# Decoder layer in fp32: a feed-forward bias of six rows in four row groups, reciprocal parts on ScalarE, correction product first, second unit reordered

## Chip, cores and metric

The kernel runs on one core of a Trainium2 chip. The metric is the device time of one execution in microseconds (us). Five engines work side by side, each with its own queue: TensorE (PE, with its weight loads shown as PEld), VectorE (DVE), ScalarE (ACT), GpSimd (POOL) and SyncE (SP, which here issues most of the DMAs). An engine works through its queue in order.

## The reference

One decoder layer on x (8 x 256 tokens of 512 features), all in fp32:

```python
x = layernorm(x + self_attention(x))     # 16 heads of 128, RoPE, causal
x = layernorm(x + cross_attention(x, ctx))  # 16 heads of 32, mask, residual scale, its own norm
x = layernorm(x + ffn(x))
```

Self-attention uses a signed weight, `sign(s) * exp(|s| - max|s|)`, over its absolute sum. The feed-forward part quantises activations and weights:

```python
xq = clip(round(x * 127 / max|x|), -128, 127) / (127 / max|x|)   # one scale for each token
wq = clip(round(w / mean|w|), -1, 1) * mean|w|                   # one scale for each matrix
h = gelu(xq @ w1q.T + b1)        # 512 -> 2048
h = layernorm(h) * gamma + beta
y = quantised(h) @ w2q.T + b2    # 2048 -> 512
```

## The kernel before, in words

The 2048 tokens are 16 tiles of 128. The work has two phases.

**Self-attention** is 32 units, 8 pairs of heads times 4 pairs of batches. fp32 matrices are split in a high and a low part and multiplied in three matmuls (L146 to L148, `mm3`); the split of an x or a weight is a cast (high part, L156 or L185) and a subtraction (low part, L157 or L183). The order of work of a unit is a string of marks (`SCHED["unit"]`, L60 to L71): `Q` and `V` are projections, `s` scores, `S` the softmax's start, `x` its exponentials, `N` its normalisation (DVE, `e`, L419), `t` the transposes of the weights (PE, L426), `u` and `r` parts of RoPE, `R` its sum, and so on; a digit says which head or half. Several units are interleaved in one string. `emit` walks through it. Marks like `X0`, `XA`, `XB`, `X1`, `BY`, `BW`, `G1` are places at which `background` (L522 to L611) hangs work for later units: loads and splits of the next x, splits of the next weights. `X0` splits the first half of the next x on DVE (L156, L157), `XA` does the cast of its second half on ACT (L185) and `XB` or `X1` the subtraction on DVE (L183). The second unit, `ui == 1`, has its own string, made from the general one by replacements (L633 to L637).

**Everything after** (from about 920 us) is written as steps, `S(...)`, each with one or more choices of engine, a planned cost, and the tiles that it reads and writes. A list scheduler puts the steps in order by due times (`PLAN`, L38 to L58); planned costs, due times and engine choices are constants in the code. The order that results is then binding on each engine (`in_order`, L1355). Three kinds of steps interleave:

- Cross-attention of a batch (L854 to L1011): scores (PE, L880), exponentials (ACT, L884), mask (DVE, L888), products with v and denominators (PE, L895, L911), reciprocals (DVE, L921; `rs` L923), their spread over the heads (PE `rp`, L930), the product with it (DVE, L933), split (`cT`, L951, L952), output projection (PE `xo`, L146 to L148), and for each tile a norm, residual, second norm (`acc`, L980) and the quantisation for the feed-forward part: `absmax` (DVE, L985 to L987), `inverse` (POOL, L993 to L1001), `acc * scale + magic` (ACT, L1004), clip to bf16 (DVE, L1008), transpose by DMA (SP, xT<-xq) and store to DRAM (`xqs`). L827 and L831 (PE `tp`, DVE `x1T`) transpose and split the next queries' x.
- The feed-forward tables (L1014 to L1048): quantised weights, gamma, beta, and the bias table `b1s`, built in four blocks on DVE (L1034, L1036).
- The feed-forward part of a tile (L1050 to L1162): `up` (PE, L1070, and its bias L1071), Gelu (ACT, L1075), mean (DVE, L1080), squares (ACT, L1084), rstd (POOL, L1089 to L1091), scale and shift in halves (DVE L1095 and L1108; ACT L1103, DVE or POOL L1105, POOL L1107), absolute maximum (DVE, L1111), `scale` (DVE, L1116 to L1118), quantisation to `hq` (L1124, L1125), transpose by DMA (SP, hT<-hq), `down` (PE `dn`, L1131, and the correction product, L1133), last residual and norm.

How the bias gets in: `up` accumulates integers times the weights' signs, and Gelu multiplies by the token's scale `a1s`. So b1 has to be divided by that scale. The reciprocal of a token's scale is cut in three bf16 parts, and b1 too. The parts of the reciprocal lie in columns of `xq` (512 to 639) that the DMA transposes with the rest, and so become rows of the fifth block of `x2`. Before, the first part stands in rows 0, 32 and 64 of that block, the second in 33 and 65, the third in 66, all others being zero, and `b1s` has 96 rows: 32 with the third part of b1, 32 with the second, 32 with the first. One matmul of 96 rows for each 512 columns (L1071) adds the six products.

How the correction gets in: `hq` is stored shifted by `HALF`, and `unhalf` times the column sums `csum` takes that out again; before, after the 16 products of `down`.

Of the kernel before, what the change touches and what calls it, by code (L numbers as in the profile page):

```python
# [10 lines left out]
F32 = mybir.dt.float32  # L11
# [67 lines left out]
def decoder_kernel(ctx: ExitStack, tc: tile.TileContext, a, out):  # L79
# [28 lines left out]
    def T(tag, shape, dt=F32, name=None):  # L108
        return (keep if tag in ("w", "xt") else sb).tile(shape, dt, name=name or tag, tag=tag, bufs=BUFS.get(tag, 1))
# [412 lines left out]
    def background(ui):  # L522
# [6 lines left out]
        if nx is not None and nx.hp == 0:  # L529
            if ui == 0:  # L530
                ex["BA"].append(nx.xload)
            ex["X0" if ui < 2 else "B0"].append(lambda: nx.xsplit(0))
            ex["XA"].append(lambda: x_half(nx.xt, nx.raws[1], 1, 0, nc.scalar))
            ex["XB" if ui > 1 else "X1"].append(lambda: x_half(nx.xt, nx.raws[1], 1, 1, nc.vector))
        elif nx is not None:
            ex["BA"].append(nx.load)
        if ui < 2:
# [6 lines left out]
        for n, hp, k1 in ([("wO", u.hp, "BW")] if ui else [], [] if ui > 1 else [("wO", 0, "BW")], [("wQ", u.hp + 1, "BW")], [("wK", u.hp + 1, ""), ("wV", u.hp + 1, "")])[u.bp]:  # L544
            if (ui or n == "wO") and hp < NHP:
                raws = {}
                ex["BV" if n == "wV" else "BA"].append(lambda n=n, hp=hp, raws=raws: raws.update(w=raw_load(a[n][hp])))
                if n == "wV":
                    late["wv"] = raws
                elif n == "wK":  # L550
                    def hi(raws=raws, hp=hp):
                        w = hw.setdefault(hp, {})["wK"] = T("w", [128, 2, 1024], F32R)
                        half_split(w[:, 0], w[:, 1], raws["w"], 0, nc.scalar)

                    def lo(raws=raws, hp=hp):
                        w = hw[hp]["wK"]
                        half_split(w[:, 0], w[:, 1], raws["w"], 1, nc.vector)

                    ex["G0"].append(hi)
                    ex["BX"].append(lo)  # L560
                else:
                    ex[k1].append(lambda n=n, hp=hp, raws=raws: load_hp(hp, n, raws["w"]))
        if ui in ABS:
# [67 lines left out]
    for ui, u in enumerate(units):  # L631
        spec = SCHED["unit" if ui else "first"]
        if ui == 1:  # L633
            for old, new in ((" N0 XB", ""), (" n0 m1", " n0 N0 m1"), ("Q000 s00 Q001", "Q000 Q001 s00"), (" S0 BA", " S0 BA f0- f2-"),
                             (" V0 v0", ""), (" t00", " V0 v0 t00")):
                assert old in spec
                spec = spec.replace(old, new, 1)  # L637
        emit(spec, u, units[ui - 1] if ui > 0 else None, units[ui - 2] if ui > 1 else None, background(ui))
        if ui == 0:
            in_order(["PE", "Activation", "DVE", "Pool", "SP"])  # L640
# [120 lines left out]
        nc.scalar.activation(mv[:, 1:2], mv[:, 6:7], AF.Identity, scale=1.0 / D)  # L761

    def rstd(mv):
        nc.gpsimd.tensor_scalar(mv[:, 2:3], mv[:, 1:2], EPS, None, ALU.add)
        nc.gpsimd.tensor_tensor(mv[:, 3:4], mv[:, 2:3], nhalf, ALU.pow)

    def shift(mv):
# [86 lines left out]
    def x(b):  # L854
# [80 lines left out]
        for qi in range(2):  # L935
# [29 lines left out]
            def scale1(m1=m1):  # L965
# [9 lines left out]
              rd=[m1, A], wr=[d])  # L975
            S([("DVE", 0.8, lambda d=d, m2=m2: stats(H[d], H[m2])),
               ("ACT", 2.1, lambda d=d, m2=m2, xq=xq: astats(H[d], H[m2], H[xq][:, 0:512]))], rd=[d], wr=[m2, f"{xq}/q"], new=[m2] + new(xq))
            S([("POOL-", 1.0, lambda m2=m2: rstd(H[m2]))], wr=[m2])
            S([("DVE", 0.13, lambda m2=m2: shift(H[m2]))], wr=[m2])
            S([("ACT", 0.71, lambda tt=tt, d=d, m2=m2: nc.scalar.activation(acc[:, tt], H[d], AF.Identity, bias=H[m2][:, 2:3], scale=H[m2][:, 3:4]))],  # L980
              rd=[d, m2], wr=[A])
# [6 lines left out]

            S([("DVE", 0.85, absmax)], rd=[A], wr=[f"{m2}/s"])

            def inverse(tt=tt, m2=m2, xq=xq):
                s, xq = H[m2], H[xq]
                nc.gpsimd.tensor_tensor(a1s[:, tt : tt + 1], s[:, 10:11], wscale[:, 0:1], ALU.mult)  # L993
                nc.gpsimd.memset(xq[:, 512:640], 0.0)
                inv = s[:, 12:13]
                nc.gpsimd.tensor_tensor(inv, s[:, 11:12], wscale[:, 2:3], ALU.mult)
                for n in (3, 2, 1):
                    c0 = 512 + 33 * (3 - n)
                    nc.gpsimd.tensor_copy(xq[:, c0 : c0 + 32 * n - 31 : 32], inv.to_broadcast([128, n]))
                    if n > 1:  # L1000
                        nc.gpsimd.tensor_tensor(inv, inv, xq[:, c0 : c0 + 1], ALU.subtract)  # L1001

            S([("POOL-", 2.0, inverse)], rd=[f"{m2}/s"], wr=[f"{xq}/i", f"a1s:{tt}"], new=new(xq))
            S([("ACT", 0.71, lambda tt=tt, d=d, m2=m2: nc.scalar.activation(H[d], acc[:, tt], AF.Identity, bias=magic, scale=H[m2][:, 11:12]))],  # L1004
              rd=[A, f"{m2}/s"], wr=[d])
            S([(e, us, lambda tt=tt, g=g: g.tensor_tensor(acc[:, tt], acc[:, tt], H["b2b"], ALU.add))
               for e, us, g in (("POOL", 1.3, nc.gpsimd), ("DVE+", 0.65, nc.vector))], rd=["b2b"], wr=[A])
            S([("DVE+", 0.36, lambda d=d, xq=xq: nc.vector.tensor_scalar(H[xq][:, 0:512], H[d], MAGIC + 127.0, -MAGIC, ALU.min, ALU.add))],  # L1008
# [5 lines left out]
    def ffn_tables():  # L1014
        unit[0] = ("w", 0)
        for wi in range(2):
            key = f"fw{wi}"
            mk(key, "xt", [128, 8192], (BF16, F16)[wi])
            for c in range(4):
                cs = slice(2048 * c, 2048 * c + 2048)  # L1020
                load(key, wq_s[wi][:, cs], 2.8, rd=["ks3:0"], part=f"/{c}", f=lambda t, cs=cs: t[:, cs])
        for n in ("g2", "be2"):
            mk(n, "w", [128, 2048])
            load(n, a[n].to_broadcast([128, 2048]), 5.0, rd=["ks2:3"])
        mk("b1s", "w p4", [96, 2048], BF16)
        for c in range(4):
            r, cs = f"b1r{c}", slice(512 * c, 512 * c + 512)
            mk(r, "p2", [96, 512])
            load(r, a["b1"][:, cs].to_broadcast([96, 512]), 1.1, rd=["ks2:3"])

            def rows(r=r, cs=cs):
                t, b1s = H[r], H["b1s"]
                for n in (96, 64, 32):
                    nc.vector.tensor_copy(b1s[0:n, cs], t[0:n])  # L1034
                    if n > 32:
                        nc.vector.tensor_tensor(t[0 : n - 32], t[0 : n - 32], b1s[0 : n - 32, cs], ALU.subtract)  # L1036
# [12 lines left out]

    def ffn(tt):  # L1050
# [10 lines left out]
        for g in range(2):  # L1061
            ps = f"up{tt}{g}"
            bank(ps, "D", [128, 1024])

            def up(g=g, ps=ps):
                for c in range(2):
                    o = H[ps][:, 512 * c : 512 * c + 512]
                    f0 = 1024 * g + 512 * c
                    for k in range(4):
                        nc.tensor.matmul(o, H[x2][:, k], H["fw0"][:, 2048 * k + f0 : 2048 * k + f0 + 512], start=k == 0, stop=False)  # L1070
                    nc.tensor.matmul(o, H[x2][0:96, 4], H["b1s"][:, f0 : f0 + 512], start=False, stop=True)  # L1071

# [40 lines left out]

        def scale():
            s = H[st]
            nc.vector.tensor_tensor(s[:, 8:9], s[:, 8:9], s[:, 9:10], ALU.max)  # L1116
            nc.vector.tensor_scalar(s[:, 8:9], s[:, 8:9], EPS, 1.0 / 127.0, ALU.max, ALU.mult)
            nc.vector.reciprocal(s[:, 9:10], s[:, 8:9])  # L1118

        S([("DVE", 0.3, scale)], rd=[f"{st}/x{e}" for e in range(2)], wr=[f"{st}/s"])  # L1120
# [6 lines left out]
        bank(dn)  # L1127

        def down(ks_):
            for k in ks_:  # L1130
                nc.tensor.matmul(H[dn], H[hT][:, k], H["fw1"][:, 512 * k : 512 * k + 512], start=k == 0, stop=False)  # L1131
            if 15 in ks_:
                nc.tensor.matmul(H[dn], unhalf, csum, start=False, stop=True)  # L1133

        fw1 = [f"fw1/{c}" for c in range(4)]
        if tt in PLAN["dve"]:
# [288 lines left out]
```

## Time and profile before

| | us |
|---|---|
| three runs, median (lowest to highest) | 1386.69 (1386.09 to 1386.78) |
| the profiled execution's own time | 1387.89 |
| its span | 1386.1 |

| engine | busy, us | share of the span | instructions |
|---|---|---|---|
| PE | 1346.7 | 97% | 8576 |
| DVE | 1091.8 | 79% | 2040 |
| ACT | 880.4 | 64% | 1948 |
| POOL | 782.0 | 56% | 985 |

The span is that of the profiled execution, from its first to its last instruction; the difference of 1.8 us to its time lies around it. Times in views of the profile count from the span's start. In the order-of-time view a line has the start, the busy time (of several instructions of the same kind, if it ends in a count over 1), the engine, the line of the code, the operation, out<-in with shapes, and in brackets idle time ahead of it and what ended that. A view of stretches gives the busy time of each engine in a piece of the span, then the granted TensorE clock as a share of the full one, the share of DMA and GB/s. A view of waits names what an engine waited for: the total, how often, and the longest.

### The profile page before, as it was taken

The page shows a single profiled execution, that of the slowest core. Times are in us where ns is not written, and L with a number is a line of the kernel's source. Part 1 is how long each engine was busy: PE and PEld are TensorE (multiplying, and loading weights), DVE is VectorE, ACT ScalarE, POOL GpSimd, SP SyncE. Part 2 cuts the span into 40 slices and gives each one's busy share as a digit, 9 for nine tenths or more (in the row PEclk, how much of TensorE's full clock was granted, in tenths as well). Part 3 has the DMA queues.
Part 4 walks back from the last instruction along what each step waited for, and adds up shares of the span by engine and source line. Part 5 has one row for each costly group of instructions (what it writes and reads, how often), then busy time and mean ns, then how long its engine had stood idle before and what let it go on. Part 6 is the DMA issues. An engine that isn't in the chain of part 4 may idle for free.

```text
span 1386.1 us, 23778 instructions
## 1 busy us (share of the span) xinstructions
PE 1346.7 (97%) x8576; PEld 1081.0 (78%) x8576; DVE 1091.8 (79%) x2040; ACT 880.4 (64%) x1948; POOL 782.0 (56%) x985
## 2 busy tenths in 40 slices
PE   9899999999999999999999999999999999988896
PEld 7789988898889888998889888888667667543342
DVE  6877768778767888887877876868767877798997
ACT  4666776776776666666665666633644445576995
POOL 5656556656666666766665665525033324376764
PEclk9999999999999999999999999999999999999999
DMA  8442342234322244223422342225324424214453
GB/s 309 182 185 109 116 178 107 92 114 165 121 76 96 92 143 176 104 84 124 189 88 99 126 175 107 69 99 191 114 59 126 140 68 143 86 34 94 113 116 99
DMA packets 85046, 170.13 MB, mean 123 GB/s; under 512 B 47040, under 2 KB 57024, under 8 KB 80064
## 3 DMA queue, kind: packets, MB, share of 16 engines
q1 hardware_dynamic: 82624, 165.99, 35.1%
q10 hardware_dynamic: 2304, 2.62, 0.7%
q8 instruction: 68, 1.11, 0.3%
q14 instruction: 50, 0.41, 0.1%
HBM read 130.31 MB, written 27.79 MB: 114 GB/s over the span
## 4 chain that ended last, share of the span: by engine, by line
PE 82%; DVE 10%; POOL 3%; ACT 2%; issue 2%; DMA 1%; SPq 0%; POOLq 0%; ACTq 0%; DVEq 0%
PE ppj L146 12%; PE ppj L147 12%; PE ppj L148 12%; PE pz L146 3%; PE pz L148 3%; PE pz L147 3%; PE pwt L426 3%; PE sc L880 3%; PE den L911 2%; PE av L895 2%; PE ppo L146 2%; PE ppo L147 2%; PE ppo L148 2%; PE psc L376 2%; PE pz L449 2%
## 5 line engine op out<-in xcount | busy, mean ns | idle before, releaser
L324 POOL TENSOR_TENSOR sw<-sw,stab 128x512 f32<-128x512 f32 x128 | 170.2, 1329 | 101.5 <-ACT sw L315 101.0
L146 PE MATMUL ppj<-xt,w 128*128 128x512 f32 x528 | 209.0, 396 | 0.3 <-ACT xt L285 0.3
L147 PE MATMUL ppj<-xt,w 128*128 128x512 f32 x528 | 206.5, 391 | 1.0 <-DVE xt L157 0.4
L148 PE MATMUL ppj<-xt,w 128*128 128x512 f32 x528 | 206.2, 391 | 0.0
L146 PE MATMUL ppj<-w,xt 128*128 128x256 f32 (+1 forms) x528 | 157.2, 298 | 1.1 <-DVE u L320 1.1
L348 POOL TENSOR_TENSOR rh<-u,rh 128x512 fp32r<-128x512 f32 x64 | 97.6, 1526 | 99.8 <-PE ppj L148 88.2
L148 PE MATMUL ppj<-w,xt 128*128 128x256 f32 (+1 forms) x528 | 152.0, 288 | 0.0
L147 PE MATMUL ppj<-w,xt 128*128 128x256 f32 (+1 forms) x528 | 151.9, 288 | 0.0
L320 DVE SCALAR_TENSOR_TENSOR u<-ppj,bqk,ctab 128x512 f32<-128x512 f32 x128 | 95.5, 746 | 70.9 <-ACT sw L315 70.6
L314 ACT ACTIVATE sw<-ppj,bqk 64x512 f32<-64x512 f32 x128 | 87.8, 686 | 92.7 <-PE ppj L148 87.9
L332 POOL TENSOR_TENSOR u<-u,sw 128x256 f32<-128x256 f32 (+1 forms) x128 | 130.8, 1022 | 0.3 <-DVE u L320 0.2
L419 DVE SCALAR_TENSOR_TENSOR e<-aw,rd,sg 128x128 f32<-128x128 f32 (+1 forms) x256 | 126.3, 550 | 0.1
L148 PEld LDWEIGHTS ppj<-xt,w 128*128 128x128 f32 x528 | 99.2, 188 | 21.6 <-DVE w L183 0.4
L406 ACT ACTIVATE aw<-aw,nm 128x256 f32<-128x256 f32 (+1 forms) x256 | 113.2, 443 | 3.9 <-DVE nm L397 3.9
L391 POOL TENSOR_SCALAR_AFFINE_SELECT aw<-aw 128x256 f32<-128x256 f32 x128 | 59.9, 492 | 98.7 <-ACT aw L385 98.7
L453 ACT CAST z<-pz 128x512 fp32r<-128x512 f32 x64 | 37.6, 587 | 121.3 <-PE pz L449 121.3
L147 PEld LDWEIGHTS ppj<-xt,w 128*128 128x128 f32 x528 | 99.3, 188 | 17.9 <-DVE xt L183 0.8
L146 PEld LDWEIGHTS ppj<-xt,w 128*128 128x128 f32 x528 | 99.3, 188 | 17.1 <-ACT xt L285 0.7
L146 PEld LDWEIGHTS ppj<-w,xt 128*128 128x128 f32 x528 | 101.9, 193 | 2.0 <-DVE u L320 1.4
L147 PEld LDWEIGHTS ppj<-w,xt 128*128 128x128 f32 x528 | 102.0, 193 | 0.6
L148 PEld LDWEIGHTS ppj<-w,xt 128*128 128x128 f32 x528 | 101.7, 193 | 0.7
L385 ACT ACTIVATE aw<-psc 128x384 f32<-128x384 f32 x128 | 62.3, 487 | 60.6 <-PE psc L148 59.9
(283 smaller groups left out, 3937.0 us busy)
## 6 DMA issues: line engine op xcount, KB each, us to landing
xt<-xs SPq DMA_DIRECT2D x28, 2048.0 KB, 8.2
xs<-xt SPq DMA_DIRECT2D x4, 2048.0 KB, 12.9
raw<-w1T SPq DMA_DIRECT2D x16, 512.0 KB, 9.5
raw<-w2T SPq DMA_DIRECT2D x16, 512.0 KB, 9.6
acc<-xn SPq DMA_DIRECT2D x4, 1024.0 KB, 8.5
raw<-wO SPq DMA_DIRECT2D x8, 512.0 KB, 9.6
wq<-wqt SPq DMA_DIRECT2D x16, 256.0 KB, 2.4
kx<-ks SPq DMA_DIRECT2D x8, 512.0 KB, 4.9
```

Of the source, the lines that this page charges most:

```text
L146: nc.tensor.matmul(ps, lh, rh, start=first, stop=False)
L147: nc.tensor.matmul(ps, lh, rl, start=False, stop=False)
L148: nc.tensor.matmul(ps, ll, rh, start=False, stop=last)
L314: nc.scalar.activation(sw[0:64], ps[64:128], AF.Identity, bias=bias[64:128])
L320: nc.vector.scalar_tensor_tensor(v3(u), v3(self.ps.pop((h, i))), self.bias(h, i), ctab.to_broadcast([128, 2, 256]), ALU.add, ALU.mult)
L324: nc.gpsimd.tensor_tensor(v3(sw), v3(sw), stab.to_broadcast([128, 2, 256]), ALU.mult)
L332: nc.gpsimd.tensor_tensor(u, u, sw, ALU.add)
L348: (nc.gpsimd if i else nc.vector).tensor_tensor(lo, u if i else u[:, :, 128:256], f32(hi), ALU.subtract)
L385: nc.scalar.activation(aw[:, h], sc3, AF.Abs, scale=1.0 / math.sqrt(DH))
L391: nc.gpsimd.affine_select(aw[:, :, blk], aw[:, :, blk], pattern=[[0, 2], [-1, 128]], compare_op=ALU.is_ge, fill=MASKED, base=0, channel_mu ...
L406: nc.scalar.activation(aw[:, h, blk], aw[:, h, blk], AF.Exp, bias=nm[:, h, i : i + 1], accum_out=rd[:, h, i : i + 1])
L419: nc.vector.scalar_tensor_tensor(e[:, h, blk], aw[:, h, blk], rd[:, h, i : i + 1], sg[:, h, blk], ALU.mult, ALU.mult)
```

## The change

1. **Second unit.** In the string of `ui == 1`, the split of the first half of the next x (`X0`) goes from behind `R00` to behind `N1`, the cast of the second half (`XA`) behind `H11`, its subtraction from `X1` to `BY`; `N0`, `L00` and `u10` go ahead of `m1`, and `x0` ahead of `H00`. The split of wO in this unit becomes two parts, the cast on ACT at `G1` and the subtraction on DVE at `BW`.
2. **Bias table.** b1 lies in rows 32c to 32c + 31 for the columns 512c to 512c + 511 (c = 0 to 3), so `b1s` is 128 x 512 with 528 columns of work space in place of 96 x 2048. In each group six rows hold parts of b1: rows 1, 3, 5 the first part, 2 and 4 the second, 0 the third. Masks for these rows are sums of columns of the identity.
3. **Reciprocal parts.** They are made on ACT, in the step after L1004, six columns in each of four groups. The POOL step stays in the plan with nothing in it; its memset moves into the step `rstd` of the same tile.
4. **Up.** The bias product of 512 columns uses six rows of its row group; both of a half come behind the eight other products.
5. **Down.** The correction product comes first.
6. **Small ones.** `rstd`: add EPS becomes times 1.0 plus EPS. `scale`: a maximum of two and a maximum with EPS become one instruction, the multiplication another.

The planned costs, due times and engine choices stay as they are, and so does the order of the steps on each engine.

```diff
-            ex["XB" if ui > 1 else "X1"].append(lambda: x_half(nx.xt, nx.raws[1], 1, 1, nc.vector))
+            ex["XB" if ui > 1 else "BY" if ui else "X1"].append(lambda: x_half(nx.xt, nx.raws[1], 1, 1, nc.vector))
...
-                elif n == "wK":
+                elif n == "wK" or ui == 1:
...
-                    ex["G0"].append(hi)
-                    ex["BX"].append(lo)
+                    ex["G0" if n == "wK" else "G1"].append(hi)
+                    ex["BX" if n == "wK" else "BW"].append(lo)
...
-            for old, new in ((" N0 XB", ""), (" n0 m1", " n0 N0 m1"), ("Q000 s00 Q001", "Q000 Q001 s00"), (" S0 BA", " S0 BA f0- f2-"),
+            for old, new in ((" N0 XB", ""), (" L00 n0 m1", " n0 N0 L00 u10 m1"), (" H01 u10 R10", " H01 R10"), (" H00 x0 a11 XA", " x0 H00 a11"), (" R00 X0", " R00"), (" N1 X1", " N1 X0"),
+                             (" l0 k10 k11 BX", " XA l0 k10 k11 BX"), ("Q000 s00 Q001", "Q000 Q001 s00"), (" S0 BA", " S0 BA f0- f2-"),
...
-        nc.gpsimd.tensor_scalar(mv[:, 2:3], mv[:, 1:2], EPS, None, ALU.add)
+        nc.gpsimd.tensor_scalar(mv[:, 2:3], mv[:, 1:2], 1.0, EPS, ALU.mult, ALU.add)
...
-            S([("POOL-", 1.0, lambda m2=m2: rstd(H[m2]))], wr=[m2])
+            def rstd_zero(m2=m2, xq=xq):
+                rstd(H[m2])
+                nc.gpsimd.memset(H[xq][:, 512:640], 0.0)
+
+            S([("POOL-", 1.0, rstd_zero)], wr=[m2])
...
-                nc.gpsimd.tensor_tensor(a1s[:, tt : tt + 1], s[:, 10:11], wscale[:, 0:1], ALU.mult)
-                nc.gpsimd.memset(xq[:, 512:640], 0.0)
+            S([("POOL-", 2.0, lambda: None)], rd=[f"{m2}/s"], wr=[f"{xq}/i", f"a1s:{tt}"], new=new(xq))
+
+            def rounded(tt=tt, d=d, m2=m2, xq=xq):
+                s, s_xq = H[m2], H[xq]
+                xq4 = s_xq[:, 512:640].rearrange("p (g r) -> p g r", g=4)
+                nc.scalar.activation(H[d], acc[:, tt], AF.Identity, bias=magic, scale=s[:, 11:12])
                 inv = s[:, 12:13]
-                nc.gpsimd.tensor_tensor(inv, s[:, 11:12], wscale[:, 2:3], ALU.mult)
-                for n in (3, 2, 1):
-                    c0 = 512 + 33 * (3 - n)
-                    nc.gpsimd.tensor_copy(xq[:, c0 : c0 + 32 * n - 31 : 32], inv.to_broadcast([128, n]))
+                nc.scalar.activation(inv, s[:, 11:12], AF.Identity, scale=wscale[:, 2:3])
+                for c0, n in ((0, 3), (3, 2), (5, 1)):
+                    nc.scalar.copy(xq4[:, :, c0 : c0 + n], inv.rearrange("p (g r) -> p g r", g=1).to_broadcast([128, 4, n]))
                     if n > 1:
-                        nc.gpsimd.tensor_tensor(inv, inv, xq[:, c0 : c0 + 1], ALU.subtract)
+                        nc.scalar.activation(inv, s_xq[:, 512 + c0 : 513 + c0], AF.Identity, scale=-1.0, bias=inv)
+                nc.scalar.activation(a1s[:, tt : tt + 1], s[:, 10:11], AF.Identity, scale=wscale[:, 0:1])
...
-            load(r, a["b1"][:, cs].to_broadcast([96, 512]), 1.1, rd=["ks2:3"])
+            r, ps_ = f"b1r{c}", slice(32 * c, 32 * c + 32)
+            mk(r, "p2", [128, 512])
+            load(r, a["b1"][:, 512 * c : 512 * c + 512].to_broadcast([32, 512]), 1.1, rd=["ks2:3"], f=lambda t, ps_=ps_: t[ps_])
...
-                for n in (96, 64, 32):
-                    nc.vector.tensor_copy(b1s[0:n, cs], t[0:n])
-                    if n > 32:
-                        nc.vector.tensor_tensor(t[0 : n - 32], t[0 : n - 32], b1s[0 : n - 32, cs], ALU.subtract)
+                t, b1s, part, m = H[r][ps_], H["b1s"][ps_, 0:512], H["b1s"][ps_, 512:1024], H["b1s"][ps_, 1024:1040]
+                for i, rs_ in enumerate(((1, 3, 5), (2, 4), (0,))):
+                    mi = m[:, 4 * i : 4 * i + 2].bitcast(F32)
+                    nc.vector.tensor_reduce(mi, ident[ps_, rs_[0] : 128 : 32], AX.X, ALU.add)
+                    for q_ in rs_[1:]:
+                        nc.vector.tensor_reduce(m[:, 12:14].bitcast(F32), ident[ps_, q_ : 128 : 32], AX.X, ALU.add)
+                        nc.vector.tensor_tensor(mi, mi, m[:, 12:14].bitcast(F32), ALU.add)
+                    nc.vector.tensor_copy(part, t)
+                    if i < 2:
+                        nc.vector.tensor_tensor(t, t, part, ALU.subtract)
+                    if i:
+                        nc.vector.scalar_tensor_tensor(b1s, part, mi, b1s, ALU.mult, ALU.add)
+                    else:
+                        nc.vector.tensor_scalar(b1s, part, mi, None, ALU.mult)
...
-                    nc.tensor.matmul(o, H[x2][0:96, 4], H["b1s"][:, f0 : f0 + 512], start=False, stop=True)
+                for c in range(2):
+                    r = 32 * (2 * g + c)
+                    nc.tensor.matmul(H[ps][:, 512 * c : 512 * c + 512], H[x2][r : r + 6, 4], H["b1s"][r : r + 6, 0:512], start=False, stop=True)
...
-            nc.vector.tensor_tensor(s[:, 8:9], s[:, 8:9], s[:, 9:10], ALU.max)
-            nc.vector.tensor_scalar(s[:, 8:9], s[:, 8:9], EPS, 1.0 / 127.0, ALU.max, ALU.mult)
+            nc.vector.tensor_scalar(s[:, 8:9], s[:, 8:9], s[:, 9:10], EPS, ALU.max, ALU.max)
+            nc.vector.tensor_scalar(s[:, 8:9], s[:, 8:9], 1.0 / 127.0, None, ALU.mult)
...
+            if 0 in ks_:
+                nc.tensor.matmul(H[dn], unhalf, csum, start=True, stop=False)
             for k in ks_:
-                nc.tensor.matmul(H[dn], H[hT][:, k], H["fw1"][:, 512 * k : 512 * k + 512], start=k == 0, stop=False)
-            if 15 in ks_:
-                nc.tensor.matmul(H[dn], unhalf, csum, start=False, stop=True)
+                nc.tensor.matmul(H[dn], H[hT][:, k], H["fw1"][:, 512 * k : 512 * k + 512], start=False, stop=k == 15)
```

More of the change, by code (lines that the diff above doesn't have):

```diff
@@ L549, in background, with hi, lo @@
                     late["wv"] = raws
-                elif n == "wK":
-                    def hi(raws=raws, hp=hp):
-                        w = hw.setdefault(hp, {})["wK"] = T("w", [128, 2, 1024], F32R)
+                elif n == "wK" or ui == 1:
+                    def hi(raws=raws, hp=hp, n=n):
+                        w = hw.setdefault(hp, {})[n] = T("w", [128, 2, 1024], F32R)
                         half_split(w[:, 0], w[:, 1], raws["w"], 0, nc.scalar)
-                    def lo(raws=raws, hp=hp):
-                        w = hw[hp]["wK"]
+                    def lo(raws=raws, hp=hp, n=n):
+                        w = hw[hp][n]
                         half_split(w[:, 0], w[:, 1], raws["w"], 1, nc.vector)
-                    ex["G0"].append(hi)
-                    ex["BX"].append(lo)
+                    ex["G0" if n == "wK" else "G1"].append(hi)
+                    ex["BX" if n == "wK" else "BW"].append(lo)
                 else:
@@ L989, in x @@
             S([("DVE", 0.85, absmax)], rd=[A], wr=[f"{m2}/s"])
-            def inverse(tt=tt, m2=m2, xq=xq):
-                s, xq = H[m2], H[xq]
-                nc.gpsimd.tensor_tensor(a1s[:, tt : tt + 1], s[:, 10:11], wscale[:, 0:1], ALU.mult)
-                nc.gpsimd.memset(xq[:, 512:640], 0.0)
+            S([("POOL-", 2.0, lambda: None)], rd=[f"{m2}/s"], wr=[f"{xq}/i", f"a1s:{tt}"], new=new(xq))
[3 more added lines that the diff above has]
+                nc.scalar.activation(H[d], acc[:, tt], AF.Identity, bias=magic, scale=s[:, 11:12])
                 inv = s[:, 12:13]
-                nc.gpsimd.tensor_tensor(inv, s[:, 11:12], wscale[:, 2:3], ALU.mult)
-                for n in (3, 2, 1):
-                    c0 = 512 + 33 * (3 - n)
-                    nc.gpsimd.tensor_copy(xq[:, c0 : c0 + 32 * n - 31 : 32], inv.to_broadcast([128, n]))
+                nc.scalar.activation(inv, s[:, 11:12], AF.Identity, scale=wscale[:, 2:3])
+                for c0, n in ((0, 3), (3, 2), (5, 1)):
+                    nc.scalar.copy(xq4[:, :, c0 : c0 + n], inv.rearrange("p (g r) -> p g r", g=1).to_broadcast([128, 4, n]))
                     if n > 1:
[L1001 to L1005, printed above, removed]
+                        nc.scalar.activation(inv, s_xq[:, 512 + c0 : 513 + c0], AF.Identity, scale=-1.0, bias=inv)
+                nc.scalar.activation(a1s[:, tt : tt + 1], s[:, 10:11], AF.Identity, scale=wscale[:, 0:1])
+            S([("ACT", 0.71, rounded)], rd=[A, f"{m2}/s"], wr=[d])
             S([(e, us, lambda tt=tt, g=g: g.tensor_tensor(acc[:, tt], acc[:, tt], H["b2b"], ALU.add))
@@ L1024, in ffn_tables, with rows @@
             load(n, a[n].to_broadcast([128, 2048]), 5.0, rd=["ks2:3"])
-        mk("b1s", "w p4", [96, 2048], BF16)
+        mk("b1s", "w p4", [128, 1040], BF16)
         for c in range(4):
-            r, cs = f"b1r{c}", slice(512 * c, 512 * c + 512)
-            mk(r, "p2", [96, 512])
-            load(r, a["b1"][:, cs].to_broadcast([96, 512]), 1.1, rd=["ks2:3"])
-            def rows(r=r, cs=cs):
-                t, b1s = H[r], H["b1s"]
-                for n in (96, 64, 32):
-                    nc.vector.tensor_copy(b1s[0:n, cs], t[0:n])
-                    if n > 32:
-                        nc.vector.tensor_tensor(t[0 : n - 32], t[0 : n - 32], b1s[0 : n - 32, cs], ALU.subtract)
+            r, ps_ = f"b1r{c}", slice(32 * c, 32 * c + 32)
+            mk(r, "p2", [128, 512])
+            load(r, a["b1"][:, 512 * c : 512 * c + 512].to_broadcast([32, 512]), 1.1, rd=["ks2:3"], f=lambda t, ps_=ps_: t[ps_])
+            def rows(r=r, ps_=ps_):
+                t, b1s, part, m = H[r][ps_], H["b1s"][ps_, 0:512], H["b1s"][ps_, 512:1024], H["b1s"][ps_, 1024:1040]
[12 more added lines that the diff above has]
+                        nc.vector.tensor_scalar(b1s, part, mi, None, ALU.mult)
             S([("DVE+", 2.5, rows)], wr=[r, f"b1s/{c}"], new=new("b1s"))
```

## The prediction

> **What bounds the kernel now.** I read the page's busy shares and its chain that ended last first, then the busy time by stretches, then the waits and the order in time of single engines wherever the change touches something.
>
> From the page, the busy line and the chain:
> ```profile
> PE 1346.7 (97%) x8576; PEld 1081.0 (78%) x8576; DVE 1091.8 (79%) x2040; ACT 880.4 (64%) x1948; POOL 782.0 (56%) x985
> PE 82%; DVE 10%; POOL 3%; ACT 2%; issue 2%; DMA 1%; SPq 0%; POOLq 0%; ACTq 0%; DVEq 0%
> ```
> TensorE sets most of the time, but 18% of the chain lies on DVE, POOL, ACT and waits for issue. The busy time by stretches says where (from:to, length, then PE, PEld, DVE, ACT, POOL):
> ```profile
> 25.00:50.00 25.00, 19.72 (x95) 15.15 (x96) 16.45 (x26) 15.53 (x38) 19.12 (x19) 0.93 0.56 204
> 1050.00:1075.00 25.00, 25.00 (x184) 18.23 (x187) 18.86 (x35) 12.78 (x19) 10.62 (x22) 1.00 0.52 149
> 1250.00:1275.00 25.00, 19.87 (x78) 8.04 (x78) 20.17 (x33) 14.66 (x18) 16.27 (x20) 0.86 0.46 96
> 1350.00:1375.00 25.00, 19.12 (x98) 8.37 (x95) 24.62 (x44) 17.52 (x21) 13.13 (x19) 1.00 0.43 95
> ```
> Three regimes. Early on, PE has gaps (unit 1 lies here). From 50 to about 1213 us it has none (25.00 of 25): there DVE work costs nothing until PE waits for it, then it costs in full. From 1213 on, DVE is the bound (24.62 of 25), with POOL and ACT handing it work; around 1250 even DVE idles.
>
> **The bias table.** Four blocks, each a step whose order on DVE is fixed. The first one, on DVE, with what stands behind it:
> ```profile
> 1062.33 0.42 DVE L1034 CAST b1s<-b1r 96x512 bf16<-96x512 f32 x1
> 1062.78 0.69 DVE L1036 TENSOR_TENSOR b1r<-b1r,b1s 64x512 f32<-64x512 f32 x1
> ...
> 1064.67 0.41 DVE L1034 CAST b1s<-b1r 32x512 bf16<-32x512 f32 x1
> 1065.01 1.40 DVE L888 TENSOR_SCALAR pt<-pt,mkf 128x1024 f32<-128x1024 f32 x2
> 1066.33 0.67 DVE L831 TENSOR_TENSOR x1T<-tp,x1T 128x512 fp32r<-128x512 f32 x1
> ```
> Fewer partitions don't make an operation shorter: 96 and 32 rows both take 0.41 to 0.42, so 32 rows for all saves nothing. A block takes 2.68 (1062.33 to 1065.01). The new one has 17 operations: three casts and two subtractions as before (2.68), a TENSOR_SCALAR (nearest: L1008, 0.42, start to start 0.45), two SCALAR_TENSOR_TENSOR of 512 (L972, 0.74) and nine of one element per row: six reductions (nearest L1216, 0.174) and three additions (L986, 0.154). The last nine are the unknown: the reciprocal L987 at 1243.03 reads what L986 at 1242.84 wrote and starts 0.19 behind it; L768 at 1243.11, which reads nothing of either, starts 0.08 behind. So nine cost 0.7 if none depends on another and 1.7 if all do. The new form adds 0.45 + 1.4 + 0.7 to 1.8 = 2.6 to 3.6 us; as most depend on the one before I take 3.2.
>
> [...]
>
> What is behind a block? On PE at that time:
> ```profile
> 1066.18 1.15 PE L880 MATMUL sc<-qst,kx 32*128 32x256 f32 x16
> 1067.26 1.07 PE L911 MATMUL den<-pt,esel 128*32 128x256 f32 x16
> ```
> In PE's fixed order the matmuls from 1067.26 need the x1T that DVE ends at 1067.01: 0.25 us of slack. A block that is 3.2 longer makes PE wait 2.95. Second block (1073.62): DVE is 6.4 late when it ends L952 (1076.97 before), needed by xo L148 at 1078.48 (slack 1.51): PE is 4.9 late. There DVE has an idle spell of 3.11 up to 1080.08, which waits for an exponential of ACT behind an earlier matmul, so its lag falls back to about 3. Third block (1082.57): 6.3 late, slacks of 1.69 (d L972, 1086.52 to 1088.22) and 1.19 (x1T, 1090.64 to 1091.83): PE 5.1. Fourth (1095.36): 9.5 late at rs L923 (1106.19), slack 1.73 to rp at 1107.92: PE 7.8. The kernel has no PE gap afterwards in which that would be made up before 1213. By 2.6 a block the same walk gives 6, by 3.6 with less idle time to absorb it 12. One of today's four blocks already met POOL (the fourth's L1036: 1.79 for 0.68), and 17 operations meet it more often: **I take +9.** Nothing but these slacks and the idle spell hides it. The smaller b1 loads (64 for 192 KB, 4.0 us to land today) are not waited for.
>
> **Reciprocals' parts.** Per tile POOL loses seven small operations and keeps the memset, now inside the rstd step. ACT gains seven: nearest L760, L761, 0.19 to 0.20; 0.12 from start to start there, and by estimate twice that where each reads the one before: 0.85 to 1.7, taken 1.4. The memset (0.20) stands earlier in POOL's queue and could wait there for its slot's last transpose: 0 to 0.5, in the bounds below. Before 1213 ACT has room (12.78 of 25), but an exponential (L884) that stands behind it reaches PE later; slacks there are 0.24 to 3. Much of that falls on a PE that is already late: **+0.5** (0 to 3). In the tail it is POOL that gains:
> ```profile
> 1243.41 1.08 POOL L996 TENSOR_TENSOR mb<-mb,wscale 128x1 f32<-128x1 f32 x1
> 1244.55 1.14 POOL L999 CAST xq<-mb 128x3 bf16<-128x3 f32 x1
> ...
> 1250.39 1.18 POOL L1001 TENSOR_TENSOR mb<-mb,xq 128x1 f32<-128x1 f32 x1
> ...
> 1252.31 4.65 POOL L1107 TENSOR_TENSOR h<-h,be 128x1024 f32<-128x1024 f32 x2
> ```
> Operations of one element take over 1 us each beside DVE's. Two tiles' worth (1243.12 to 1246.75 and 1247.98 to 1252.31, 8 us) stand ahead of two additions (L1107, 2.33 each) for which DVE waits, and, through xq, ahead of SP's transposes, behind which hT<-hq waits (hq was done at 1238.9, issue at 1255.39) and then PE. Two of DVE's and PE's waits of 1222 to 1276:
> ```profile
> DVE fs L1111 <- POOL h L1107: 3.0, 1, 3.0
> PE dn L1131 <- DMA hT<-hq: 4.8, 1, 4.8
> ```
> Without them the second L1107 could end near 1251.6 instead of 1256.96. All DVE idle time of this stretch is 6.5; 3.0 + 0.5 of it ends by POOL. ACT's additions (2 x 1.4 ahead of the gelus at 1246 to 1250) give up to 2 back; ACT's idle 6.14 us behind them (1251.4 to 1257.6) takes the rest. Earlier transposes let PE's dn start earlier, which shortens what later tiles wait for. Bounds -2 and -7, **taken -4.5**. Next late is DVE itself: from 1276 to 1372 it idles only some 2 us, so more isn't to be had.
>
> **Unit 1.** The split of unit 2's x (L156 0.86, L157 2.20) leaves DVE's queue at 36.40 and comes back after L419 of 52.60. PE's waits of 41 to 48 us (line, releaser: total, times, longest):
> ```profile
> PE pwt L426 <- DVE e L419: 2.6, 3, 1.6
> PE ppj L146 <- DVE u L320: 1.1, 1, 1.1
> ```
> These 3.76 us go or shrink: L320 at 39.42 comes at 37.7, the V projection of 47.84 can start near 43.9; ACT's half of the split (L185, 1.04 at 43.64) goes back too and stands no longer ahead of L314. The cast half of wO's split passes from DVE to ACT (0.86 there, about 1.04 here), where 4.47 us of idle time before 56.12 takes it. The half-clock spell behind them (47.84 to 53.55, 0.21 a matmul where 0.12 is usual) may shrink too. But the split now ends near 55.0 to 55.6, and unit 2's first projection needs it: 1 to 1.6 us of new wait; the second half (L183, 1.21) follows it and costs some 1.3 more. Equal work stands 0 to 1.7 earlier: **-0.8** (bounds -3 with a full clock, +1 if L157 stays at its contended 2.20). The later load of unit 3's x (issue near 55, use near 61, landing 6.0 us at the median of such loads) just fits and is in the upper bound.
>
> **Up, down, small ones.** The two K=96 bias matmuls of a half become K=6 in different row groups. PE's 32-row products (1066.18 above) start 0.068 apart where 256 columns at 0.12 are usual in 128 rows, so the pair may overlap and save up to 0.2 per half; only four halves (1202.77 to 1223.94) stand where PE is the bound or near it. Nothing to -0.8. The correction product first takes its 0.22 into the wait for hT; at the end it is worth 0.2 at most. Together **-0.3**. A two-operand scalar operation on POOL or DVE costs what the other did (L1116 0.16, L1117 0.15): 0.
>
> [...]
>
> **Sum.** -0.8 + 9 + 0.5 - 4.5 - 0.3 = **+3.9**. On the profiled execution (1387.89, span 1386.1) that is 1391.8; it lay 1.2 above the median of the runs, 1386.69, so for a median I forecast **1390.6**. The measurement tells 0.2% (2.8 us) from no change.
>
> **Rivals.**
> - Faster: the nine small operations slip between the large ones for nothing and DVE's idle time of 1050 to 1110 takes more. A block then adds 1.9, PE ends the stretch 3 late, and with -7 in the tail and -1.5 in unit 1 the sum is -5.5: 1381 to 1383. It decides where a block adds less than about 1.5 us over PE's slack. For: PE's slack is 1.2 to 1.7 behind three of the four. Against: 0.45 + 1.4 us are read from rows. 25%.
> - Much slower: 3.6 a block with POOL in the way (+12), ACT's parts ahead of the exponentials (+2), nothing from unit 1, -3 in the tail: +11, 1395 to 1399. 20%.
> - No difference: PE is 8 late but the DVE work that doesn't need PE catches up meanwhile, so that the tail gives back all: 1384 to 1389. 10%.
> - My forecast, 1387 to 1394: 45%, of which 7 points lie within 0.2% and 38 above.
>
> Faster 25 + 2 = 27%, the same 7 + 8 = 15%, slower 58%. The range takes in most of both outer rivals: 1381.5 to 1398; the forecast's own is 1387 to 1394.
>
> **What would show it.** Each new block's length on DVE (5.3 to 6.4) and PE waits for DVE between 1067 and 1108, none before; the first `up` (1202.84) 5 to 10 us later; no POOL inverse, and L1107's counterpart followed by DVE without a 3 us wait near 1260; PE's waits near 44 us gone and new ones for the split near 55. I am wrong if the new blocks stay under 4 us, if PE shows no wait for DVE there, or if unit 1's stall moves instead of shrinking.

## The result, and the profile after

Slower: 1406.51 us median (1404.01 to 1407.49, four runs) against 1386.74 (1386.09 to 1387.63): a ratio of 1.0139 [1.0124, 1.0154], +19.8 us where +3.9 was forecast. The direction was right; the time lies far above the range of 1381.5 to 1398. The profiled execution took 1407.49, its span is 1405.3. Line numbers of after are larger by 1 in cross-attention, by 5 at the tile's quantisation (L980 is L985) and by 16 in most of the feed-forward part (L1107 is L1123).

The page's busy line and the stretches (from:to, length, then PE, PEld, DVE, ACT, POOL, PE's granted clock, DMA share, GB/s):
```profile
PE 1353.9 (96%) x8564; PEld 1077.6 (77%) x8576; DVE 1104.0 (79%) x2087; ACT 905.6 (64%) x2061; POOL 749.4 (53%) x873
```
```profile
25.00:50.00 25.00, 20.54 (x107) 15.73 (x108) 14.63 (x24) 15.12 (x39) 18.84 (x20) 1.00 0.49 183
1050.00:1075.00 25.00, 21.94 (x158) 15.49 (x157) 16.53 (x35) 13.86 (x29) 6.70 (x4) 0.93 0.44 117
1100.00:1125.00 25.00, 21.22 (x132) 13.84 (x130) 18.73 (x42) 13.57 (x29) 2.38 (x5) 0.83 0.52 153
1250.00:1275.00 25.00, 15.55 (x58) 4.98 (x57) 23.20 (x38) 21.40 (x47) 16.43 (x20) 0.80 0.26 65
```
The stretch of 1100 to 1125 in the trace of before:
```profile
1100.00:1125.00 25.00, 24.72 (x223) 16.83 (x222) 14.57 (x26) 14.84 (x23) 4.34 (x12) 1.00 0.35 91
```
Between 1050 and 1125 PE had one gap of 0.3 us before; now it has about 9 us of gaps, and its clock is no longer 1.00 there.

To see where the time comes from I set each instruction's start against the same one in the trace of before ("lag"). PE runs 1.3 us ahead up to 1055; by 1125 it is 16.1 behind, so 17.4 us are lost in that stretch. From there to 1226 it loses 1.5 more, and the last 160 us, where the forecast had a gain of 4.5, end at a lag of 19.2. PE's waits of 1045 to 1145 (line, releaser: total, times, longest):
```profile
PE sc L881 <- ACT pt L885: 2.2, 2, 1.9
PE kvp L146 <- DVE kvs L803: 1.9, 1, 1.9
PE xo L148 <- DVE cT L953: 1.5, 1, 1.5
PE qp L146 <- ACT kvs L797: 1.2, 1, 1.2
PE den L912 <- ACT pt L885: 1.1, 1, 1.1
```
With the four shorter ones they sum to 9.2. So 8 of the 17.4 us aren't waits. Most of them are matmuls at half clock: three spells, 3.41, 3.41 and 6.83 us long, in which products of 512 columns start 0.43 apart instead of 0.23, so that they cost at most half their length, 6.8; the last 1.4 us aren't put down to anything. Parts of the second and the third spell (the clock is the third number from the end; `...` marks lines left out):
```profile
1106.40:1109.80 3.40, 3.40 (x9) 2.62 (x9) 3.30 (x11) 0.00 (x0) 0.20 (x1) 0.53 0.92 330
...
1120.00:1123.40 3.40, 3.40 (x20) 2.19 (x24) 1.96 (x4) 2.33 (x3) 0.00 (x0) 0.50 0.19 66
1123.40:1126.80 3.40, 3.40 (x21) 1.96 (x14) 2.94 (x5) 0.00 (x0) 0.00 (x0) 0.52 0.00 0
```

The first loss lies ahead of every bias block. In order of time, first on ACT, then on DVE:
```profile
1050.91 0.28 ACT L1003 ACTIVATE mb<-mb,wscale 128x1 f32<-128x1 f32 x1
1051.27 0.21 ACT L1005 CAST xq<-mb 128x12 bf16<-128x12 f32 x1
...
1052.71 0.80 ACT L985 ACTIVATE acc<-d,mb 128x512 f32<-128x512 f32 x1
```
```profile
1053.55 0.69 DVE L990 TENSOR_REDUCE mb<-acc 128x1 f32<-128x512 f32 x1 [2.07 <-ACT acc L985]
...
1057.58 0.68 DVE L803 TENSOR_TENSOR kvs<-kvp,bvb 128x512 f32<-128x512 f32 x1
```
The seven small ACT operations take 1.8 us from the first to the next tile's L985. DVE waits 2.07 us for that L985, a second tile's parts follow on ACT, and DVE comes late to the kvs operation that empties the PSUM bank PE needs at 1058.31. The first bias block on DVE is 5.24 us long:
```profile
1064.88 0.14 DVE L1040 TENSOR_REDUCE b1s<-ident 32x1 f32<-32x4 f32 x1
1064.95 0.14 DVE L1042 TENSOR_REDUCE b1s<-ident 32x1 f32<-32x4 f32 x1
1065.12 0.15 DVE L1043 TENSOR_TENSOR b1s<-b1s 32x1 f32<-32x1 f32 x1
...
1069.45 0.74 DVE L1048 SCALAR_TENSOR_TENSOR b1s<-b1s 32x512 bf16<-32x512 bf16 x1
1070.12 0.73 DVE L889 TENSOR_SCALAR pt<-pt,mkf 128x1024 f32<-128x1024 f32 x1
```
Independent small ones start 0.07 apart, dependent ones 0.17 to 0.18. The four blocks are 5.24, 5.38, 5.55 and 5.47 long, against 2.68, 2.68, 3.22 and 3.79 before: +2.56 for the first and 9.3 for all four, or 2.3 a block, where the forecast allowed 2.6 to 3.6. No operation of a block is longer than 0.75 us in this trace, where before a cast (0.96 for 0.42) and a subtraction (1.79 for 0.68) were lengthened.

### The profile page after: what moved, and what is told of

Read it like the earlier page. It is cut to its first block, busy times and chain, and to the rows that moved or that the text cites. A ratio compares the mean times of both kernels' runs of the same rounds, so it can differ in the third digit from the quotient of the medians.

```text
span 1405.3 us, 23834 instructions
## 1 busy us (share of the span) xinstructions
PE 1353.9 (96%) x8564; PEld 1077.6 (77%) x8576; DVE 1104.0 (79%) x2087; ACT 905.6 (64%) x2061; POOL 749.4 (53%) x873
## 5 line engine op out<-in xcount | busy, mean ns | idle before, releaser
L147 PEld LDWEIGHTS ppj<-xt,w 128*128 128x128 f32 x528 | 99.3, 188 | 19.2 <-DVE xt L157 1.6
L146 PEld LDWEIGHTS ppj<-w,xt 128*128 128x128 f32 x528 | 100.7, 191 | 2.4 <-DVE u L320 0.8
L147 PEld LDWEIGHTS ppj<-w,xt 128*128 128x128 f32 x528 | 101.0, 191 | 0.6
L148 PEld LDWEIGHTS ppj<-w,xt 128*128 128x128 f32 x528 | 100.7, 191 | 0.7
```

What stands on the lines that cost most here:

```text
L146: nc.tensor.matmul(ps, lh, rh, start=first, stop=False)
L147: nc.tensor.matmul(ps, lh, rl, start=False, stop=False)
L148: nc.tensor.matmul(ps, ll, rh, start=False, stop=last)
```

## The experiments

**The second unit's order alone** (the kernel before with the diff's first part):

> Only the second unit's new order on the kernel before. In the changed kernel PE ran 0.87 us ahead of the kernel before from 75 us to 950 us. If that order is the cause, this kernel is 0.9 us faster (1385.8), PE is 0.87 ahead at 900 us and nothing changes behind it. The rival, that the lead comes or goes with something later: within 0.3 us of the kernel before.

1386.43 against 1386.99: 0.9996 [0.9987, 1.0005]. Nothing is shown. Its PE waits of 41 to 62 us sum to 2.8 instead of 3.7, but in the changed kernel to 3.9. And the lead of PE isn't evidence of the order: the kernel without parts below has the old order, its PE is 1.7 us ahead at 75 us, and its waits there are those of before. What differs is the half-clock spell beside these waits: it lasts from 46.75 to 53.58 in the trace of before, from 46.61 to 50.03 in that one. The lag in the first 75 us differs by that much between executions of the same code. Over all traces the spell is 6.83, 6.83 and 3.41 us long with the old order; with the new one it's missing in three, 3.41 in five and 6.83 in one. That it tends to be shorter isn't ruled out. Up to 1.8 us of gain (the interval) stays possible, the forecast's 0.8 among it.

**Reciprocal parts back on POOL**, bias table and the rest as in after (`...` in these excerpts marks what is left out):
```diff
-                nc.scalar.activation(inv, s[:, 11:12], AF.Identity, scale=wscale[:, 2:3])
+                nc.gpsimd.tensor_tensor(inv, s[:, 11:12], wscale[:, 2:3], ALU.mult)
                 for c0, n in ((0, 3), (3, 2), (5, 1)):
-                    nc.scalar.copy(xq4[:, :, c0 : c0 + n], ...)
+                    nc.gpsimd.tensor_copy(xq4[:, :, c0 : c0 + n], ...)
...
```

> The changed kernel with the reciprocals' parts back on POOL (same six columns in four groups, memset back beside them). My theory now: the parts on ACT are what cost most, since 1.8 us of small ACT instructions per tile stand ahead of what PE waits for, and each PE gap of some 2 us brings 3.4 us of half clock. Then the bias blocks alone (2.56 us more each on DVE, as the changed kernel shows) make PE 4 to 6.5 late by 1125 us, hardly any half clock in 1050 to 1125, and the time is 1389 to 1393. The rival, that the bias table makes the 17 us of 1050 to 1125 by DVE alone: 1402 to 1406.

1396.37: 1.0067 [1.0054, 1.0079], +9.4 us. Both expectations missed: the bias table alone costs neither 4 nor 17. PE loses 10.9 us from 1050 to 1125 (lag -1.8 to 9.1), 6.9 of it waits; one wait alone, near 1110, is 3.3 us, and 6.5 us are lost around it: a half-clock spell of 6.83 us begins within that wait. The 3.4 us of half clock in the theory are those behind the gap of 1.91 in after.

**Bias table and `up` of before**, parts on ACT (in the columns of before):
```diff
-                for c0, n in ((0, 3), (3, 2), (5, 1)):
...
+                for n in (3, 2, 1):
+                    c0 = 512 + 33 * (3 - n)
+                    nc.scalar.copy(s_xq[:, c0 : c0 + 32 * n - 31 : 32], inv.to_broadcast([128, n]))
...
+                    nc.tensor.matmul(o, H[x2][0:96, 4], H["b1s"][:, f0 : f0 + 512], start=False, stop=True)
...
```

> The changed kernel with the bias table and its matmuls of before; the parts still on ACT, in the columns of before. My theory: PE is 3.9 late near 1058 as in the changed kernel, half a clock included, and 1 to 4 more by 1125: +5 to +8 there, and 0 to +2 behind 1226: 1391 to 1397. The rival (bias table alone): PE under 2 late by 1125, time at most 1389.

1394.04: 1.005 [1.0037, 1.0062], +7.1 us. As my theory had it: PE loses 3.8 us near 1058 and 1.5 more up to 1125 (lag -2.0 to 3.4), and behind 1226 about another 3, more than the 0 to 2 expected; DVE's lag grows by 2.8 between 1245 and 1255, where its operations lie beside POOL's additions as in the next run. The forecast's term for this was +0.5, and a gain of 4.5 in the tail. The two parts together, 9.4 + 7.1, leave 3.3 of the 19.8 us to what they do to each other; that rest I haven't split. Both figures also hold the second unit's order and the small changes, which weren't measured one by one.

**The parts left out**, on the kernel before (the bias then stays out of the feed-forward part):
```diff
-                inv = s[:, 12:13]
-                nc.gpsimd.tensor_tensor(inv, s[:, 11:12], wscale[:, 2:3], ALU.mult)
-                for n in (3, 2, 1):
...
```

> The kernel before without the three parts of the reciprocal (the bias is left out of the feed-forward part that way; POOL still makes the token's scale and the memset). It shows what it is worth in the last 170 us to free POOL of this work, with nothing put on ACT. The forecast's step: 3 to 4.5 us less behind 1226, 1382 to 1384. My theory now: DVE's wait for POOL goes, but DVE's two-input operations run beside POOL's additions and are 2 to 3 times as long, so 0 to 2 us are gained, 1384.7 to 1386.7.

1389.11: 1.0016 [1.0007, 1.0025]. Less work, nothing put on ACT, and 2.1 us slower: worse than either expectation. DVE and POOL in its trace:
```profile
1248.22 2.84 DVE L999 TENSOR_TENSOR acc<-acc,b2b 128x512 f32<-128x512 f32 x1
...
1251.06 3.29 DVE L1101 SCALAR_TENSOR_TENSOR h<-h,fs,be 128x1024 f32<-128x1024 f32 x1
```
```profile
1248.05 5.22 POOL L1100 TENSOR_TENSOR h<-h,be 128x1024 f32<-128x1024 f32 x2 [2.12 <-DVE h L1098]
```
POOL's two additions now start at 1248.05 instead of 1252.31, as the forecast wanted. But there they lie beside two DVE operations with two inputs from SBUF, which take 2.84 for 0.67 and 3.29 for 1.28, 4.2 us more. Before, DVE waited 3.04 us for POOL; now it doesn't wait, and is slower by more than that: its lag goes from -2.3 to -0.3 between 1245 and 1255 and stays there to the end. The same two rows stand in the trace of after:
```profile
1268.59 2.83 DVE L1011 TENSOR_TENSOR acc<-acc,b2b 128x512 f32<-128x512 f32 x1
...
1271.42 3.29 DVE L1124 SCALAR_TENSOR_TENSOR h<-h,fs,be 128x1024 f32<-128x1024 f32 x1
```
In the trace without the parts the two DVE operations end 0.55 and 1.08 us behind the two POOL additions (1250.51 and 1253.27); in the trace of before, with no addition beside them, they take 0.67 and 1.28. What makes them longer isn't shown.

**The same with these two POOL additions on DVE** (tiles 1 and 2):
```diff
+    ONDVE = (1, 2)
...
-            S([("POOL", 2.4, lambda: nc.gpsimd.tensor_tensor(H[h][:, lo], H[h][:, lo], H["be2"][:, lo], ALU.add))], ...)
+            S([("POOL", 2.4, lambda: (nc.vector if tt in ONDVE else nc.gpsimd).tensor_tensor(...))], ...)
```

> The kernel before without the parts (1389.1, the bias left out that way) with the two POOL additions that met DVE's two-input operations near 1250 done on DVE instead, at the same place in the order: DVE 2.4 us more, and nothing on POOL beside L1006 and L1108 of these tiles. If the meeting is what costs, the 4.2 us by which these two were longer go: 1386 to 1387.5. The rival, that they are long for another reason: 1390.5 to 1392.

1387.32: 1.0002 [0.9993, 1.001]; 1.8 us less than without this, as expected. DVE has 2.4 us more to do, and the two operations are short again:
```profile
1250.24 0.68 DVE L999 TENSOR_TENSOR acc<-acc,b2b 128x512 f32<-128x512 f32 x1
1250.84 1.22 DVE L1102 TENSOR_TENSOR h<-h,be 128x1024 f32<-128x1024 f32 x1
...
1252.05 1.28 DVE L1103 SCALAR_TENSOR_TENSOR h<-h,fs,be 128x1024 f32<-128x1024 f32 x1
```
DVE's lag hardly moves between 1245 and 1255 (-0.3 to -0.2), where it lost 2.0 without this. So the meeting with POOL is the cause of that loss. Freeing POOL of the parts is worth nothing here, with or without it.

**The ACT parts two steps later**, on the changed kernel: the same seven operations recorded just ahead of the tile's transpose.
```diff
+            def turned(xq=xq, xT=xT, parts=parts):
+                parts()
+                nc.sync.dma_start_transpose(H[xT], H[xq])
```

> The changed kernel (1406.5), with the seven ACT instructions of a tile recorded two steps later, just ahead of the tile's transpose, so that they stand in ACT's queue behind what PE and DVE wait for. If their place is what costs, most of the 7 us that they cost alone goes: no PE wait for kvs near 1058, 1397 to 1401. The rival, that it is ACT's time as such, or that the transposes become late instead: 1404 to 1408.

1404.36: 1.0127 [1.0113, 1.0141]. Each theory had a part. Near 1058 PE now loses 0.95 us instead of 3.86, and 12.7 instead of 17.4 up to 1125; but 1.7 more are lost near 1160, and DVE falls from a lag of 13 (1215) to 18 (1255). About 2 of that is the meeting with POOL, as in after; late transposes can have a part in the rest (PE waits 12.2 us between 1222 and 1280 for the loads of `xqs` that follow them, 9.4 in after), which isn't shown. Their place decides what they hit first; moving them this way isn't a cure.

**Is it the clock?** Two fillings of the 3.3 us gap near 1110, on the kernel with the parts on POOL. First, 14 matmuls over 32 rows with weights of zero:
```diff
+                    if (bp, m) == (2, 2):
+                        for i in range(14):
+                            nc.tensor.matmul(H[ps], H["one"][64:96], H[x1][64:96, 0, 0], start=False, stop=i == 13)
```

> The kernel with the parts back on POOL (1396.4). There PE has one gap of 3.3 us near 1110, and lags 6.5 more behind it: half its clock for what follows. Here 14 matmuls that add zeros to the projection just ahead of the gap fill it (3.2 us of PE). If the rest of the 6.5 is the clock that PE's idle time brings, the clock stays at 1.00, PE lags 5 to 7 at 1125 instead of 9.1, and the time is 1393 to 1395, although PE does more. The rival, that the matmuls behind the gap are slow because of late operands: 1396 to 1399.

1396.18: 1.0067 [1.0054, 1.008], no difference. PE's wait is gone, yet the clock falls all the same:
```profile
1110.20:1113.60 3.40, 3.19 (x20) 2.06 (x18) 1.78 (x6) 3.30 (x5) 1.93 (x8) 1.00 0.01 2
1113.60:1117.00 3.40, 3.40 (x20) 2.18 (x24) 2.09 (x4) 2.43 (x3) 0.00 (x0) 0.52 0.57 145
```
Without the filling:
```profile
1113.60:1117.00 3.40, 3.40 (x22) 2.30 (x24) 1.92 (x3) 2.52 (x4) 0.00 (x0) 0.50 0.58 147
1117.00:1120.40 3.40, 3.40 (x23) 1.84 (x19) 3.14 (x6) 0.00 (x0) 0.00 (x0) 0.76 0.00 0
```
With it the spell is half as long (3.41 us for 6.83), behind the filling and a gap of 0.21, and PE's lag at 1125 is 8.3 instead of 9.1, but the time doesn't show it. Either the clock follows something other than a busy PE (few rows, or zeros), or it wasn't the idle time. Second, the projection ahead of the gap computed twice, 12 matmuls over 128 rows with data:
```diff
-                    for k in range(4):
+                    for k in [*range(4), *range(4)] if (bp, m) == (2, 2) else range(4):
```

> The kernel with the parts back on POOL (1396.4) and another filling of PE's gap of 3.3 us near 1110: the projection ahead of it is computed twice (12 more matmuls over all 128 rows, 2.75 us; the second pass starts its sums anew). The zeros of 32 rows in the run before this one kept PE busy, but its clock still fell to 0.50 behind them. If what counts is how much of the array works, the clock stays at 1.00 here, PE's lag at 1125 falls from 9.1 by 3 to 4, and the time is 1392.5 to 1393.5. The rival, that the half clock has nothing to do with what stands ahead: 1396 to 1397.

1393.58: 1.0044 [1.0031, 1.0056]; 2.8 us less than without it, although PE does more:
```profile
1110.20:1113.60 3.40, 2.79 (x14) 1.70 (x12) 1.93 (x6) 3.07 (x4) 2.05 (x8) 1.00 0.00 0
1113.60:1117.00 3.40, 3.20 (x34) 2.07 (x35) 2.98 (x5) 2.67 (x4) 0.00 (x0) 1.00 0.66 147
```
In the stretch 1113.6 to 1117 the clock is 1.00 instead of 0.50, and PE's lag at 1125 is 7.0 instead of 9.1. Of what the bias table costs, 2 to 3 us are thus the clock behind this one gap. In the trace of after a spell came behind a gap of 1.91 us (ahead of 1058.31, behind 32-row products), and one behind gaps of 0.40 and 1.22 (ahead of 1103.74 and 1105.61), while none came behind one of 1.49 (ahead of 1084.01). What starts a spell isn't shown.

**The bias table once for all 128 rows**, parts on POOL: the four groups lie in different rows, so one pass over 128 rows does the work of four blocks.
```diff
+            for c in range(4):
+                nc.sync.dma_start(H["b1s"][32 * c : 32 * c + 32, 1024:2048].bitcast(F32), a["b1"][:, 512 * c : 512 * c + 512].to_broadcast([32, 512]))
...
+            rows = (lambda: None) if c == 0 else (lambda c=c: b1_part(c - 1))
```

> The kernel with the parts back on POOL (1396.4), but the bias table made once for all 128 rows instead of four times for 32: four loads into one tile, then its three passes (2.0, 2.0 and 1.2 us by the rows of the changed kernel) in the places of the second, third and fourth block, nothing in the first. If PE's lag of 10.9 us there is the price of DVE work in these places, 5.2 us instead of today's 10.8 and 21 make PE as early as with the old table or earlier: no waits of PE on these steps, 1385 to 1388. The rival, that the new `up`, `down` or the other small edits hold part of it: 1389 or more.

1385.21: 0.9988 [0.9979, 0.9997], faster than both kernels by the interval, if little. PE's only wait for these engines between 1050 and 1130 is 0.3 us, and its lag stays at -1.5 there. What the second unit, the new `up` and the new `down` add to that isn't separated; the pair of bias matmuls takes 0.39 us together, where each took 0.38.

**The same with the two additions on DVE:**

> The fastest so far (1385.2: bias table in one pass, parts on POOL) with the same two additions on DVE. DVE's wait of 3.0 us for them goes and 2.4 us of DVE work comes; later steps that waited for POOL come earlier: 1383.5 to 1385. If the wait only moves to another step: 1386 to 1387.5.

1386.48: 0.9995 [0.9986, 1.0004]. The 3.1 us wait for POOL is gone from DVE's waits, and 2.4 us of work, a new wait of 0.9 for PE and one of 1.4 instead of 1.1 for ACT stand in its place. No gain: the wait moved, as the expectation's second case had it.

## Why the prediction was wrong, point by point

- **What bounds the kernel**: right. In PE's stretch what a late DVE or ACT step went beyond its slack cost PE in full, and more by the clock (17.4 us lost with 9.2 of waits); the three regimes hold after too.
- **Bias table, +9**: measured alone +9.4 in time and 10.9 in PE's lag. The size was right, partly by luck, since the working misses in both directions. The blocks add 2.3 on average in after, 2.5 with the parts on POOL, instead of 3.2, and they aren't lengthened by meeting POOL more often: in after only one small addition (0.31 for 0.15, beside POOL's L953 of 1087.19), the fourth (6.33) with the parts on POOL. Its first step misread a need: it had `den` of 1067.26 wait for x1T, with 0.25 us of slack. In after that `den` starts at 1071.00, ahead of x1T (1071.45) and just behind the mask operation of 1070.12, and PE loses 1.3 us there, not 2.95. Behind the third block PE is 4.4 late with the parts on POOL (5.1 forecast); the other 6.5 fall around the one wait of 3.3, and 2 to 3 of them (by the double projection) are PE's clock, which the walk nowhere has.
- **Reciprocals' parts on ACT, +0.5**: the step that failed first. It said that much of it "falls on a PE that is already late". The first two tiles' parts stand near 1051 to 1057, 8 us ahead of the first bias block, where PE isn't late; their 2 x 1.8 us came to PE, with the half-clock spell behind the wait of 1.91, as 3.8 us. Up to 1125 they cost 5.3, and 7.1 us in the whole with the tail. The row price was also low: 1.8 us a tile, not 1.4.
- **Relief in the tail, -4.5**: the second failed step. It took the 3.04 us that DVE waited for POOL as time to be had, and let POOL's additions end near 1251.6, so start near 1246.9, without asking what DVE does just then: two-input operations, 4.2 us longer beside them. Of the small POOL operations that it read as over 1 us each, four of fourteen took 1.08 to 1.27, the others 0.19 to 0.55. Without any ACT work the relief is no gain but a loss of 2.1 us. The first of the two additions also waits for the L1105 that starts at 1247.98 and ends at 1249.19, so it couldn't have started near 1246.9.
- **Unit 1, -0.8**: not decided; within 0.1% of nothing. Its waits sum to 3.9 us instead of 3.7 in after: they moved, which the forecast had named as a sign of being wrong.
- **Up, down, small ones, -0.3**: the pair of 6-row matmuls does overlap (0.39 for two, from 0.38 for each), and a half of `up` takes 2.22 from start to end instead of 2.34. What that brings in time can't be told apart here. A two-operand scalar step took 0.19 on POOL (0.22 before with one operand) and 0.21 on DVE (0.15 before for the maximum), so it wasn't quite the same on either.
- **Signs**: PE's waits of 1067 to 1108 came as forecast, but one came at 1058.31 too, where none was to be, and the first `up` is 17 us later instead of 5 to 10. DVE's wait for POOL is gone as forecast, without the gain that it was to stand for.
- **Rivals**: "much slower" had ACT's parts dear and less relief, which was right, and POOL in the way of the blocks, which wasn't; it stopped at +11, since it had neither the clock nor a loss in the tail.

## What to carry to other kernels

Where one engine is busy without gaps, price a delay not only by slack but also by the half-clock spells that can follow its gap: here 17.4 us were lost with 9.2 of waits, and up to 6.8 of the rest lies in such spells. An engine's wait for another isn't free time: before counting it as gain, look at which operations will lie side by side once it goes. Small operations "on an engine with room" count by what stands behind them in its queue; find the first place where they stand, not the average.

## What the runs showed of the hardware

- PE's granted clock was 1.00 or 0.50 in the traces of before (five spells of 0.50) and after (eight); but for the last of each, in which the trace ends, they lasted 3.41 or 6.83 us. The length of a gap alone didn't decide: in after, gaps of 1.91, of 0.40 and 1.22, and of 1.95 us were followed by spells, one of 1.49 was not, and in the first 75 us the same code had a spell of 6.83 in one execution and of 3.41 in another.
- A spell also came behind 3.46 us of uninterrupted matmuls over 32 rows with weights of zero and a gap of 0.21, but not behind 2.75 us of 128-row ones with data and gaps of 0.60 and 0.21. Whether rows or zeros matter wasn't tried.
- A DVE operation with two SBUF inputs beside a POOL addition of 128x1024 (2.34 to 2.35 us in before; 2.46 and 2.79 in after) took 2.83 or 2.84 and 3.29 us for 0.67 and 1.28, in all four traces in which POOL was freed of the parts and kept the additions; with the additions on DVE it took 0.68 and 1.28.
- DVE operations took about as long on 32 rows (after) as on 128 (the table made in one pass): the cast of 512 columns 0.41 to 0.42 and 0.41 to 0.43 us, the subtraction 0.68 to 0.69 and 0.69.
